# Decoder layer with attention, cross-attention and experts: two reorderings at the seams between its stages

## The chip, the core and the metric

The kernel runs on one core of one Trainium2 chip. The metric is the device time of one execution in microseconds (us). Its engines are named as the profile names them: PE (matrix multiplication; PEld is its weight load), DVE (vector), ACT (activation), POOL (GpSimd), and SP, which only issues DMAs. Matrices pass through PE as 32-bit floats, so each product of the program is two passes in the profile's counts (a transpose is one).

## What is computed

`x` is a batch of 8 sequences of 512 positions and 256 features. Three blocks follow each other, each adding its output to `x`:

```
x = x + attn(layernorm(x))                 # 16 heads, causal window of 128, 16 global positions
x = x + xattn(layernorm(x), ctx)           # 16 heads, 64 context positions, mask
x = x + ffn(layernorm(x))

def ffn(x):                                # S = 8, B = 512: attention over the 8 sequences
    y = layer_norm(x + mha(x), g1, be1)    # 4 heads
    idx = argmax(y @ Wg.T)                 # one of 8 experts for each of 4096 rows
    out = for each row: relu(y @ W1[idx] + b1[idx]) @ W2[idx] + b2[idx]
    return layer_norm(y + out, g2, be2)
```

The attention of the third block runs across the 8 sequences at one position, so it works on groups of 16 positions (8 x 16 = 128 rows).

## The kernel before

**Stages.** The first stage goes through the 8 sequences: self-attention and, one sequence behind, cross-attention. Each finished sequence is written to a DRAM tensor `x2d`; the last one in two halves (`HALVES`). The second stage, the blocks, takes 64 positions of all sequences at a time (`NBLK` = 8 blocks of `NG` = 4 groups): `block_start` loads nothing itself but normalises the rows and makes q, k and v, `group` is the attention of one group, `block_end` does the layer norm, the choice of the expert, and the scatter of each row to its expert's place in the DRAM tensor `rows_d`. The third stage, the expert tiles, takes 128 rows of one expert at a time: `expert_tile(i)` gathers them, loads W1, transposes, multiplies by W1 (L1281), takes the relu on ACT and DVE (L1286, L1288), multiplies by W2 (L1296), normalises and scatters to the output. It begins once the first four blocks are scattered and runs between the later groups.

**What sets the order.** Every piece of work is a Python generator that is started at a step number (`works`) and goes on to its next `yield` once a step (`in_steps`). What it yields is its rank in the next step: `PREFIX` 0, `TURN` 1, `VALUES` 2, `SMALL` 3, `SCORES` 4, `OTHER` 5, `EXPS` 6, `LOADS` 7; lower ranks come first, and among equals the piece begun last. The order so made is the order of each engine's queue: `in_order` adds a dependency from each instruction of PE, DVE, ACT and POOL to the one before it on its engine. SP's DMAs keep the program's order as well.

**The first seam.** The last half of the last sequence ends at steps `F0 + 1` to `F0 + 3` in `context_end`: the sums `den` (L723) on PE, three filler matmuls (`keep_busy(3)`, L286), the reciprocal `rd` on DVE (L732), a product that makes two columns of it, `rz`, on POOL (L735), its spreading over the partitions `ri` on PE (L750), the product `xoT` on DVE (L760), the output projection on PE (L198) and its sum on DVE (L446). Between these stands `block_start(0)`: it begins at step `F0`, does nothing in it, and in step `F0 + 1`, at rank `LOADS`, makes the statistics (`statistics`: L157, L159, L160 on DVE, the power on POOL at L161) and the normalised rows `fxn` (L168 on DVE), and issues the loads of block 2. In step `F0 + 2` come four filler matmuls (`keep_busy(4)`) and the transposes of `fxn` (L186), which ACT copies out (L188). Block 0's rows come by four loads of 112 rows each (L847) and one load of the last sequence's 16 rows for all groups (L852), which waits for the first half's write to `x2d`.

**The second seam.** Tile 0 begins at step `F0 + 35`. Its transposes (L1270) are in step `F0 + 37` and its first products (L1281) in step `F0 + 38`, at rank `EXPS`, so behind that step's group work on PE: the transposes of one group's probabilities (L983, which wait for POOL's product L978), another's values (L989), the experts' logits of block 5 (L1019) and the output projection of a third (L198). In the same step, at rank `TURN`, are tile 1's transposes. Ahead of the first products stands the read of the expert's number into a register of PE (L1274).

Of the kernel before, what the change touches and what calls it, by code (L numbers as in the profile page):

```python
# [41 lines left out]
PREFIX, TURN, VALUES, SMALL, SCORES, OTHER, EXPS, LOADS = range(8)  # L42
# [58 lines left out]
def decoder_kernel(ctx: ExitStack, tc: tile.TileContext, a: dict, out: bass.AP):  # L101
# [48 lines left out]
    def statistics(src):  # L150

        n = src.shape[1]
        st = small.tile([P, NG, 6], F32, tag="st")
        mv = small.tile([P, NG, 2], F32, tag="mv")
        rs = small.tile([P, NG], F32, tag="rs")
        for i in range(n):
            nc.vector.bn_stats(st[:, i, :], src[:, i, :])  # L157
        for i in range(n):
            nc.vector.bn_aggr(mv[:, i, :], st[:, i, :])  # L159
        nc.vector.tensor_scalar(rs[:, :n], mv[:, :n, 1], EPS, None, ALU.add)  # L160
        nc.gpsimd.tensor_tensor(rs[:, :n], rs[:, :n], nhalf[:, :n], ALU.pow)  # L161
        return mv, rs

    def normalised(dst, src, mv, rs, g=None, be=None):
        for i in range(src.shape[1]):
            m, r = mv[:, i, 0:1], rs[:, i : i + 1]
            if g is None:
                nc.vector.tensor_scalar(dst[:, i, :], src[:, i, :], m, r, ALU.subtract, ALU.mult)  # L168
            else:
                nc.vector.scalar_tensor_tensor(  # L170
                    dst[:, i, :], src[:, i, :], m, g, ALU.subtract, ALU.mult
                )
                nc.vector.scalar_tensor_tensor(
                    dst[:, i, :], dst[:, i, :], r, be, ALU.mult, ALU.add
                )
# [45 lines left out]
    if True:  # L221
# [60 lines left out]
        def keep_busy(n):  # L282

            ps = ps_m.tile([P, 512], F32, tag="m", name="busy_ps")
            for i in range(n):
                nc.tensor.matmul(  # L286
                    ps[:, : 2 * P], ident, cst[:, C_ID : C_ID + 2 * P], start=True, stop=True
                )

        def prepared():  # L290

            for t in (vc.rearrange("p b j d -> p (b j d)"), *vzs):
                nc.vector.memset(t, 0.0)
            nc.vector.tensor_copy(upto_q, cst[:, C_TRI : C_TRI + P])
            nc.vector.tensor_scalar(xbq4, xbq, 0.25, None, ALU.mult)

            nc.vector.tensor_copy(ident_b, ident)
            nc.vector.tensor_copy(
                pre_b, cst[:PRE, C_CUR : C_CUR + PRE].unsqueeze(1).to_broadcast([PRE, 8, PRE])
            )  # L300
            for r in range(2):
                half = slice(64 * r, 64 * r + 64)
                nc.vector.tensor_copy(
                    twice_b[half], cst[half, C_ID + 64 * r :][:, :NKC].unsqueeze(1).to_broadcast([NKC, 2, NKC])
                )
            nc.vector.tensor_copy(
                selx_b, cst[:, C_SELX : C_SELX + 2 * P].rearrange("p (f k) -> p f k", f=2)
            )
            for i in range(2):
                nc.gpsimd.memset(nxs[i], 0.0)  # L310

            keep_clock(1)
            yield

        def context_keys():
            for hf in range(2):
                ps = ps_m.tile([P, 512], F32, tag="m")
                project(ps, xwk, hf * P, ctxT)
                for r, mask in enumerate((mask_e, mask_o)):
                    nc.vector.tensor_scalar(  # L320
                        kc[:, hf, :, r, :],
                        ps.rearrange("p (b k) -> p b k", k=NKC),
                        xbk[:, hf : hf + 1],
                        mask,
                        ALU.add,
                        ALU.mult,
                    )
                yield

        def context_values(bs):  # L330
            for b in bs:
                ps = ps_m.tile([P, 512], F32, tag="m")
                for r in range(2):
                    heads = slice(r * HD, (r + 1) * HD)
                    for k in range(2):
                        nc.tensor.matmul(
                            ps[r * 64 : (r + 1) * 64, :P],
                            ctxT[:, k, b * NKC : (b + 1) * NKC],
                            xwv[:, k, :].rearrange("p (j d) -> p j d", d=2 * HD)[:, :, heads],
                            start=k == 0,  # L340
                            stop=k == 1,
                        )
                for r in range(2):
                    rows = slice(r * 64, (r + 1) * 64)
                    heads = slice(r * HD, (r + 1) * HD)
                    nc.vector.tensor_tensor(
                        vc[rows, b, :, heads],
                        ps[rows, :P].rearrange("p (j d) -> p j d", d=HD),
                        xbv[rows].rearrange("p (j d) -> p j d", d=2 * HD)[:, :, heads],
                        ALU.add,  # L350
                    )
                if b % 2:
                    yield
# [423 lines left out]
        F0 = START[B] + 9  # L777
# [3 lines left out]
        works = [(3, prepared(), LOADS), (5, context_keys()), (7, context_values(range(B)))]  # L781
# [17 lines left out]
    if True:  # L799
# [75 lines left out]
        def block_start(n):  # L875

            t = blocks[n]
            yr = t["yr"]
            x2 = yr[:, :, D : 2 * D]
            xn = one.tile([P, NG, D], F32, tag="xn", name=f"fxn_{n}")  # L880
            if n == 0:

                yield LOADS
            stats = statistics(x2)
            if n:
                yield
            normalised(xn, x2, *stats)
            if n + 2 < NBLK:
                block_load(n + 2)
            yield  # L890
            xT = one.tile([P, 2, 512], F32, tag="xT", name=f"fxT_{n}")
            if n == 0:
                keep_busy(4)
            transposed(xT, xn, ps_m)

            def add_bias(g):
                nc.gpsimd.tensor_tensor(yr[:, g, :D], xn[:, g], f["bo"], ALU.add)

            add_bias(0)
            add_bias(1)  # L900
            yield
            t["q"] = qT = qsh.tile([P, 2, 512], F32, tag="qT", name=f"fq_{n}")
            kT = qsh.tile([P, 2 * ROW], F32, tag="pT", name=f"fk_{n}")[:, : 2 * 512]
            t["k"] = kT = kT.rearrange("p (f q) -> p f q", f=2)
            for hf in range(2):
                ps = ps_m.tile([P, 512], F32, tag="m")
                project(ps, f["wqkv"], hf * P, xT)
                nc.scalar.activation(
                    qT[:, hf], ps, AF.Identity, bias=f["bq"][:, hf : hf + 1], scale=0.125
                )  # L910
                ps = ps_m.tile([P, 512], F32, tag="m")
                project(ps, f["wqkv"], D + hf * P, xT)
                nc.scalar.activation(
                    kT[:, hf], ps, AF.Identity, bias=f["bqkv"][:, 2 + hf : 3 + hf]
                )
                add_bias(2 + hf)
                yield
            t["v"] = v = qsh.tile([P, NG, D], F32, tag="pc", name=f"fv_{n}")
            for gg in range(NG // 2):
                ps = ps_m.tile([P, 2, D], F32, tag="m")  # L920
                for i in range(2):
                    project_rows(ps[:, i, :], f["wqkv"], 2 * D, xT, (2 * gg + i) * P)
                nc.vector.tensor_tensor(
                    v[:, 2 * gg : 2 * gg + 2],
                    ps,
                    f["bv"].unsqueeze(1).to_broadcast([P, 2, D]),
                    ALU.add,
                )
            nc.gpsimd.tensor_copy(
                yr[:, :, 2 * D], cst[:, C_TOK + n * NG : C_TOK + (n + 1) * NG]  # L930
            )
# [281 lines left out]
        def expert_tile(i):  # L1213
# [56 lines left out]
                nc.tensor.transpose(pt[:, k, :], t[:, k * P : (k + 1) * P], ident)  # L1270
            tT = tsh.tile([P, 2, P], F32, tag="rT", name="tT")
            nc.vector.tensor_copy(tT, pt)
            yield EXPS
            e_pe = nc.tensor.value_load(eidx[0:1, j : j + 1], min_val=0, max_val=E - 1)  # L1274
            h = one.tile([P, NG, D], F32, tag=("xn", "xT")[i % 2], name=f"h_{i}")
            h = h.rearrange("p g d -> p (g d)").rearrange("p (f t) -> p f t", t=P)
# [46 lines left out]
        works += [(F0 - 18, block_weights()), (F0 - 6, norm_weights()), *((F0 - 5, block_loads(n)) for n in range(2))]  # L1323
        works += [(F0 + 5, made_room(), LOADS), (F0 + 9, expert_weights())]
        for n in range(NBLK):
            works.append((F0 + 4 * n, block_start(n)))
            for g in range(NG):
                works.append((F0 + 4 * n + 6 + g, group(n, g)))
            works.append((F0 + 4 * n + 15, block_end(n, 0, NG)))
        for k, (nb, n) in enumerate(((NB1, NT1), (NB2, NT2 - NT1), (NBLK, NT - NT2))):  # L1330
            works.append((F0 + 4 * nb + 16, make_table(f"t{k}", n, nb < NBLK)))
        for i in range(NTC):
            works.append((F0 + 4 * NB1 + 19 + i, expert_tile(i), VALUES))
# [109 lines left out]
```

## Time and profile before

| | |
|---|---|
| median of 3 runs | 1115.96 us (1115.93 to 1119.26) |
| the profiled execution's own time | 1115.88 us |
| its span, first to last instruction | 1114.1 us |
| busy: PE, DVE, ACT, POOL | 1047.9, 712.5, 580.3, 474.0 us |
| share of PE in the chain that ended last | 54% |
| the first seam, 603.0 to 617.8 us | PE busy 13.1 of 14.8 us |
| the second seam, 806.0 to 819.6 us | PE busy 11.0 of 13.6 us |

A line of a timeline gives the start in us from the span's start, the us to the end of the last of its instructions, the engine, the line of the kernel, the operation, the tile written and those read, the shapes, the count, and in brackets how long the engine was idle before it and what ended that. Ends of matmuls are modelled and overlap the next start, so the time between two starts tells more than a length. A view by stretches gives for each stretch its length, each engine's busy us with the number of its instructions, the clock granted to PE as a share of full speed, the busy share of the DMA engines and the GB/s. A releaser is inferred from semaphores. Lines are those of the kernel before; in the changed kernel they are one less from L888 on.

### The profile page before, as it was taken

How to read it: one execution, taken by the hardware profiler on the slowest of the kernel's cores; microseconds unless marked ns; L12 is line 12 of the kernel's file. 1: busy time of each engine (PE TensorE's matmuls, PEld its weight loads, DVE VectorE, ACT ScalarE, POOL GpSimd, SP SyncE). 2: the span in 40 equal slices, each digit the busy share in tenths (PEclk: the TensorE clock that was granted, in tenths of full speed). 3: DMA queues.
4: the chain of work that ended last, by engine and by line, in shares of the span. 5: the costliest groups of instructions: out<-in, count | busy, mean ns of one | idle time of the engine just before them, and what ended most of it. 6: DMA issues, size and time to landing. Idle time of an engine off the chain costs nothing.

```text
span 1114.1 us, 24420 instructions
## 1 busy us (share of the span) xinstructions
PE 1047.9 (94%) x8940; PEld 764.8 (69%) x8940; DVE 712.5 (64%) x1809; ACT 580.3 (52%) x2039; POOL 474.0 (43%) x553
## 2 busy tenths in 40 slices
PE   9798998999989999899999999999899999999994
PEld 5465665566655666666656577666678999999993
DVE  6958668497584874857853445667756675544542
ACT  2878678677686677766842456555431211111110
POOL 2152424235243262333421333455465766555552
PEclk9999999999999999999999999999999999999997
DMA  6000001010010010100003660121466877666630
GB/s 219 11 1 11 2 1 49 1 48 2 1 49 2 21 30 1 48 11 21 30 10 100 192 174 2 39 76 39 143 201 201 260 231 251 213 202 210 197 112 10
DMA packets 55824, 95.31 MB, mean 86 GB/s; under 512 B 11282, under 2 KB 39189, under 8 KB 55704
## 3 DMA queue, kind: packets, MB, share of 16 engines
q1 hardware_dynamic: 48408, 72.71, 21.1%
q0 software_dynamic: 7296, 21.02, 5.7%
q8 instruction: 73, 1.20, 0.4%
q14 instruction: 47, 0.39, 0.1%
HBM read 78.22 MB, written 17.45 MB: 86 GB/s over the span
## 4 chain that ended last, share of the span: by engine, by line
PE 54%; DVE 20%; ACT 8%; issue 4%; DMA 4%; POOL 2%; POOLq 0%; DVEq 0%; SPq 0%
PE ps L193 11%; PE hps L1281 9%; PE ps L1296 8%; PE ps L198 8%; ACT s L515 5%; DMA tb<-rows_d,t2srci 4%; DVE s L503 3%; DVE nm L511 2%; PE av L574 2%; DVE rx L530 2%; DVE nm L647 2%; PE ps L952 2%; PE xav L711 2%; PE sc L467 1%; DVE xb L446 1%
## 5 line engine op out<-in xcount | busy, mean ns | idle before, releaser
L515 ACT ACTIVATE s<-s,nm 128x144 f32<-128x144 f32 (+1 forms) x512 | 203.4, 408 | 9.2 <-DVE nm L511 9.2
L1286 ACT ACTIVATE h<-hps,b 128x128 f32<-128x128 f32 x148 | 42.3, 368 | 212.8 <-issue 184.2
L1281 PE MATMUL hps<-tT,w 128*128 128x128 f32 x1184 | 138.6, 275 | 0.1
L1281 PEld LDWEIGHTS hps<-tT,w 128*128 128x128 f32 x1184 | 135.5, 192 | 0.6 <-DMA r<-in_b 0.3
L551 POOL TENSOR_TENSOR pc<-pT,cst 128x512 f32<-128x512 f32 x96 | 123.0, 1302 | 30.4 <-DVE pT L547 29.8
L1296 PE MATMUL ps<-w,h 128*128 x592 | 133.7, 379 | 0.0
L1296 PEld LDWEIGHTS ps<-w,h 128*128 128x128 f32 x592 | 109.7, 190 | 13.4
L515 ACT ACTIVATION_READ_ACCUMULATOR s<-s,nm 128x1 f32 x512 | 101.0, 197 | 0.0
L526 POOL COPY rx<-s 128x128 f32<-128x128 f32 x48 | 14.6, 305 | 198.9 <-ACT s L515 198.9
L161 POOL TENSOR_TENSOR rs<-rs,nhalf 128x4 f32<-128x4 f32 (+1 forms) x34 | 33.5, 985 | 132.2 <-DVE rs L160 131.5
L511 DVE TENSOR_REDUCE nm<-s 128x8 f32<-128x1152 f32 (+1 forms) x64 | 84.5, 1320 | 5.5
L1288 DVE TENSOR_SCALAR h<-hps,b 128x128 f32<-128x128 f32 x148 | 41.7, 345 | 66.1 <-ACT h L1286 66.1
L467 PE MATMUL sc<-kz,qT 32*128 32x512 f32 (+1 forms) x512 | 76.0, 593 | 3.0 <-DVE s L495 2.3
L503 DVE COPY_PREDICATED s<-upto_q,sc 128x512 f32<-128x512 int32 x96 | 65.0, 731 | 19.5 <-ACT s L502 19.5
L545 PE MATMUL pt<-cst,s 128*128 128x128 f32 x512 | 72.0, 277 | 2.4 <-ACT pT L549 1.7
L502 ACT COPY s<-sc 128x512 f32<-128x512 f32 x96 | 51.7, 592 | 39.2 <-PE sc L467 39.2
L545 PEld LDWEIGHTS pt<-cst,s 128*128 128x128 f32 x512 | 59.0, 142 | 17.8 <-issue 6.9
L193 PE MATMUL ps<-fxT,w_fwqkv 128*128 128x512 f32 x128 | 58.8, 604 | 0.0
L193 PE MATMUL ps<-xT,w_wqkv 128*128 128x512 f32 x128 | 58.2, 597 | 0.0
L978 POOL TENSOR_TENSOR fs<-fs,sm 128x512 f32<-128x512 f32 x32 | 33.3, 1041 | 57.7 <-DVE sm L977 53.6
L529 DVE RECIPROCAL rc<-sm 128x8 f32<-128x8 f32 x64 | 12.6, 197 | 69.4 <-ACT s L515 69.2
L1310 POOL TENSOR_TENSOR rs<-rs,nhalf 128x1 f32<-128x1 f32 x37 | 21.5, 580 | 75.4 <-DVE rs L1309 59.6
(249 smaller groups left out, 2241.4 us busy)
## 6 DMA issues: line engine op xcount, KB each, us to landing
w<-in_W SPq DMA_DIRECT2D x45, 1024.0 KB
r<-in_b SPq DMA_DIRECT2D x37, 128.0 KB
xb<-in_x SPq DMA_DIRECT2D x7, 512.0 KB
x2d<-xb SPq DMA_DIRECT2D x7, 512.0 KB
y<-x2d SPq DMA_DIRECT2D x24, 128.0 KB
mj<-in_maskT SPq DMA_DIRECT2D x16, 128.0 KB
cst<-in_consts SPq DMA_DIRECT2D x1, 1011.0 KB
y<-x2d SPq DMA_DIRECT2D x8, 112.0 KB
```

What stands on the lines that cost most here:

```text
L193: nc.tensor.matmul(ps, w[:, k, o0 : o0 + P], xT[:, k, :], start=k == 0, stop=k == 1)
L198: nc.tensor.matmul(ps, xT[:, k, t0 : t0 + P], w[:, k, o0 : o0 + D], start=k == 0, stop=k == 1)
L467: nc.tensor.matmul(ps[j // 2][:, j % 2].rearrange("p r w k -> p r (w k)"), qT[rows[j], hf, q0 : q0 + P], kz[rows[j], hf, :, q0 + P - nw * ...
L502: nc.scalar.copy(s4, ps[jj][:, :, :, 0, :])
L503: nc.vector.copy_predicated(s4, upto_q.unsqueeze(1).unsqueeze(1).to_broadcast([P, 2, 2, P]), ps[jj][:, :, :, 1, :],)
L511: nc.vector.tensor_reduce(nm, s[:, :, :nk], AX.X, ALU.max, negate=True)
L515: nc.scalar.activation(s[:, h, :nk], s[:, h, :nk], AF.Exp, bias=nm[:, h : h + 1], accum_out=sm[:, h : h + 1],)
L545: nc.tensor.transpose(pt[:, h, :], s[:, 4 * jj + h, :P], ident)
L551: nc.gpsimd.tensor_tensor(pc[:, hs, :], pT[:, hs, :], upto_k.unsqueeze(1).to_broadcast([P, 4, P]), ALU.mult,)
L1281: nc.tensor.matmul(ps[:, f, :], w1[:, k, f * P : (f + 1) * P], tT[:, k, :], start=k == 0, stop=k == 1)
L1286: nc.scalar.activation(h[:, f, :], ps[:, f, :], AF.Relu, bias=b1[:, f : f + 1])
L1296: nc.tensor.matmul(ps, h[:, f, :], new["w2"][:, bass.ds(e_pe, 1), f, :].rearrange("p o d -> p (o d)"), start=f == 0, stop=f == NFC - 1,)
```

## The change

The first block's generator starts one step earlier, makes its statistics in step `F0`, yields, and normalises one step later, so the statistics stand ahead of the reciprocal of the last sums in DVE's queue, and the power ahead of `rz` in POOL's. Two of the four filler matmuls ahead of its transposes go. The first expert tile's generator yields `TURN` in place of `EXPS` ahead of its first products, so these stand behind tile 1's transposes and ahead of the groups' work of that step; its relu parts on ACT and DVE and its two sums on POOL (L1291, L1292) move ahead in their queues with them. The other blocks and tiles keep their ranks.

```diff
@@ block_start
             stats = statistics(x2)
-            if n:
-                yield
+            yield OTHER if n else LOADS
             normalised(xn, x2, *stats)
             if n + 2 < NBLK:
                 block_load(n + 2)
             yield
             xT = one.tile([P, 2, 512], F32, tag="xT", name=f"fxT_{n}")
             if n == 0:
-                keep_busy(4)
+                keep_busy(2)
             transposed(xT, xn, ps_m)
@@ expert_tile
             nc.vector.tensor_copy(tT, pt)
-            yield EXPS
+            yield EXPS if i else TURN
             e_pe = nc.tensor.value_load(eidx[0:1, j : j + 1], min_val=0, max_val=E - 1)
@@ works
         for n in range(NBLK):
-            works.append((F0 + 4 * n, block_start(n)))
+            works.append((F0 + 4 * n - (n == 0), block_start(n)))
```

## Prediction

> **What bounds the kernel now.** I read the page first, then the timelines of PE, DVE and POOL around the two places that the diff touches, then the stretches with their granted clock, then the landings of DMAs.
>
> The page gives PE 94% of the span:
>
> ```profile
> span 1114.1 us, 24420 instructions
> ...
> PE 1047.9 (94%) x8940; PEld 764.8 (69%) x8940; DVE 712.5 (64%) x1809; ACT 580.3 (52%) x2039; POOL 474.0 (43%) x553
> ```
>
> From 608 us to 1098.6 us, PE's last matmul, PE stands still for few moments of over 0.06 us; two clusters of them lie at the edits. A microsecond saved there reaches the end only if nothing behind it is late instead. The profiled execution took 1115.88 us, 1.78 more than its span, and the median of the three runs is 1115.96; I sum against 1115.88 and add 0.08.
>
> The first place, PE and then DVE (start, us, engine, line, tile, shape, count, idle before and what ended it):
>
> ```profile
> 606.67 1.92 PE L723 MATMUL den<-xp,cst 128*32 128x128 f32 x32
> 608.52 1.56 PE L286 MATMUL busy_ps<-cst 128*128 128x256 f32 x6
> 610.47 1.13 PE L750 MATMUL ri<-rz,cst 64*128 64x256 f32 x4 [0.39 <-POOL rz L735]
> 611.53 1.99 PE L286 MATMUL busy_ps<-cst 128*128 128x256 f32 x8
> 613.36 0.54 PE L186 MATMUL xps<-cst,fxn 128*128 128x128 f32 x2
> 614.30 0.33 PE L186 MATMUL xps<-cst,fxn 128*128 128x128 f32 x1 [0.41 <-DVE fxn L168]
> 615.03 0.76 PE L186 MATMUL xps<-cst,fxn 128*128 128x128 f32 x5 [0.40 <-DVE fxn L168]
> 615.85 1.97 PE L198 MATMUL ps<-w_xwo,xoT 128*128 128x256 f32 x8
> ```
>
> ```profile
> 608.70 0.96 DVE L732 RECIPROCAL rd<-den 64x128 f32<-64x128 f32 x1 [6.59 <-PE den L723]
> 609.70 1.41 DVE L157 BATCH_NORM_STATS2 st<-y 128x6 f32<-128x256 f32 x4
> ...
> 611.41 0.17 DVE L160 TENSOR_SCALAR rs<-mv 128x4 f32<-128x4 f32 x1
> 612.78 2.20 DVE L168 TENSOR_SCALAR fxn<-y,mv,rs 128x256 f32<-128x256 f32 x4 [1.19 <-POOL rs L161]
> 615.01 0.69 DVE L760 TENSOR_TENSOR xoT<-ri,xoT 128x512 f32<-128x512 f32 x1
> ```
>
> DVE stood idle for 6.59 us before the reciprocal, and then had the reciprocal, the statistics and the normalisation to do one behind the other while PE spent 1.83 us on filler (L286) and still waited 0.81 us for the normalised rows.
>
> The second place, PE, and the stretches with the clock (stretch; length; busy us and counts of PE, PEld, DVE, ACT, POOL; granted clock; DMA):
>
> ```profile
> 809.69 0.38 PE L1270 MATMUL pt<-cst,tb 128*128 128x128 f32 x2
> 812.29 0.70 PE L983 MATMUL pt<-cst,fs 128*128 128x128 f32 x4 [2.22 <-POOL fs L978]
> ...
> 816.53 3.73 PE L1281 MATMUL hps<-tT,w 128*128 128x128 f32 x32
> 820.10 0.38 PE L1270 MATMUL pt<-cst,tb 128*128 128x128 f32 x2
> ```
>
> ```profile
> 809.40:812.80 3.40, 1.18 (x9) 0.75 (x7) 1.12 (x5) 0.26 (x1) 2.97 (x4) 1.00 0.41 157
> 812.80:816.20 3.40, 3.40 (x29) 2.35 (x28) 0.00 (x0) 2.62 (x11) 2.61 (x3) 0.50 0.33 64
> ```
>
> PE waits 2.22 us for POOL, whose queue is full of scatters, and in the next 3.4 us its clock is granted at half, so that the groups' matmuls (L983 to L198) take 4.24 us instead of 2.66 (0.53 + 0.59 + 0.57 + 0.97, the same lines at 767.68 to 770.34). Tile 0's products then stand behind all that.
>
> **Part 1: block 0's statistics ahead of the reciprocal.** In the changed program's order only DVE's block of statistics moves past L732, POOL's L161 past L735, and two of four filler matmuls go; SP's order is the same. block_load(2) and its four DMAs keep their place.
>
> The statistics may start when block 0's last load lands. SP issues it at 604.70 and the trace's last landing record of it is at 606.96. L157 to L160 took 609.70 to 611.58, 1.88 us, with 0.05 of overlap at the end, so now 606.98 to 608.86. The denominators (L723) end at 608.66, so the reciprocal is held for some 0.1 us: 608.81 to 609.77. POOL's L161 starts 0.15 us after L160 and takes 1.01: 609.01 to 610.02. The pair L735, which used to start at 609.81, now has L161 ahead of it and starts at 610.05, 0.24 later; so `ri` starts at 610.71 instead of 610.47 (PE's wait there grows from 0.39 to 0.63) and ends at 611.77. The two fillers left take half of 1.83, to 612.69. L168 starts when L161 is done, at 610.06 instead of 612.78, and with 2.20 us ends at 612.26: all four rows are there before the fillers end, so PE's waits of 0.41 and 0.40 go. Eight transposes at 1.02 (L186 x8 elsewhere) end at 613.71; L760 follows L168 on DVE, 612.26 to 612.95, ahead of that. L198 starts at 613.71 instead of 615.85: **2.14 us**. What is late next is PE itself. The removed fillers cost nothing: what they covered is gone. If the rows were late by x, PE would wait x less the 0.43 us between 612.26 and 612.69. Bounds of this part: 0 if the load lands 2.1 us later, and 2.4 if POOL's order cost nothing.
>
> From 617 to 804 us PE is idle only at 777 and at 785 to 788, both behind DVE work that itself follows PE, so the 2.14 us travel on.
>
> **Part 2: tile 0's products ahead of the groups.** On PE the 16 products (L1281, 32 passes, 3.57 us) move from behind L198 to right behind tile 1's transposes, ahead of L983, L989, L1019 and L198. ACT's L1286 moves ahead of L984, L997, the last group's exponentials (L969) and L1029; DVE's L1288 ahead of L1002; POOL's L1291 and L1292 (0.73 + 0.68 us) ahead of a memset and a gather. Times below are on the scale of the profile of before.
>
> What the products wait for is there: tT at 809.04, W1 (landed at 787.9), the PSUM pair (exponentials done at 808.59). New is that PE's first read of the expert's number, L1274, is no longer hidden behind matmuls: its sequencer work ran from 814.01 to 815.50, 1.49 us. Begun behind tile 1's transposes, at about 809.2, it lets the products start at about 810.8; PE idles 0.7 us instead of 2.22. For the cost of this uncovered read there are two ends, nothing and the whole 1.49 behind 810.07 (811.56); either is inside the slack found below.
>
> Products 810.8 to 814.4; the four groups' lines at full clock 2.66 us, to 817.0. Then tile 2's transposes need their gather, landed at 817.17 (0.13 us to PE as at tile 0): 817.30. Then L983 needs POOL's product L978, 816.67 to 817.72, which no part of the change moves, since POOL works from 808.87 on without a PE wait: L983 at 817.78 instead of 820.32. From there to the next products took 2.62 us with an ACT wait of 0.21, of which I keep 0.1, since ACT no longer has L1286 in front: 817.78 + 2.27 is 820.05 for PE's tile 1 products, instead of 822.94: **2.89 us**. PE has 0.5 to 0.8 us in hand before POOL's 817.72, so neither the register read nor the half clock of a passing wait is needed for this number.
>
> Who is behind the new waits: ACT holds L984 to L1029 for L1286 (814.4 to 815.5), so the last exponentials end at 817.8 instead of 816.0; their reciprocal and POOL's L978 come at 821 to 822, before 822.86 to 823.9 of now. DVE's L1288 waits for ACT to 815.5 with L1002 behind it, whose matmul only ends at 817.0. The gather behind L1291 and L1292 lands at about 823.5 instead of 821.94, and is used at 827 (829.97 less 2.9). W1 of tile 2 lands at 825.9, used at 830.
>
> A rule to weigh against this: the Trainium skill, "TensorE: Matmul & The Clock Gate", Part 1, has PE fall to half clock after an idle window of about 3.4 us, and advises only against gaps longer than about 3 us. By that rule a wait of 2.22 us would not have cost the clock; the row shows that it did (busy 1.18 of 3.40, then 0.50). What follows if the half clock has another cause is a rival below.
>
> **Sum.** 1115.88 - 2.14 - 2.89 + 0.08 = 1110.9.
>
> **Rivals.**
> - *The half clock stays*, because it comes from where PE's evaluation falls and not from this wait (for it: at 505.6 the clock also is 0.50 behind a stretch in which PE was busy 2.85 of 3.40). Then 14 of the 32 passes and part of the groups' lines behind 812.8 take twice their time, about 1.7 us, less the 0.5 of slack: part 2 gives 1.7, and the time is 1112.1.
> - *A later transfer takes it back.* PE is nearly gapless behind 843 us, but tile 11's gather lands at 898.23 and is used at 898.88. If gathers there go by DMA traffic and not by PE, up to 5.0 - 0.65 = 4.4 us would return: 1111 to 1115.3, middle 1113. Against it: gathers wait for buffers that PE and DVE free, so they move too.
> - *The load is late* (the slower side). DVE takes its instructions in order: all of part 1 hangs on the load being down before the denominators. L198 starts 6.73 us after the statistics. At a landing of 609.1 part 1 is worth nothing (1113.0), at 612.0 it has eaten part 2, and behind that the kernel is slower: it would need 7.3 us from issue instead of the 2.26 traced. W1 loads in a full queue take up to 9.7 us (822.66 to 832.38), but here the queue ahead is empty.
> - *The change does not move what it says*: the program's order shows that it does, so only noise would be left, 1115.9.
>
> **How the numbers follow.** Forecast 70%, half clock 10%, transfer 9%, load late 8% (half of it still faster, a third slower), no effect 3%. Three runs spread by 3.3 us once, so I take 0.3% (3.3 us) as what can be told from no change: faster means below 1112.6. The forecast and most of the half-clock case lie there, 0.78; slower 0.03; the rest 0.19. Range: below, POOL not binding in part 2 (0.7 more) and 0.2 in part 1 give 1110.0; above, the half clock and the middle of the transfer case give 1113.5.
>
> **What would show it.** In the profile of the changed kernel: DVE's L157 about 0 to 0.2 us behind the landing and L732 behind it, `ri` 0.2 later, no wait at the first block's transposes, L198 2.1 us earlier; at the second place PE's largest wait under 1 us, granted clock 1.00 all through, L983 of tile 2's stage released by POOL, products of tile 1 5.0 us earlier than now; and the same 5 us at PE's last matmul. It is wrong if L732 starts over 0.5 us after the denominators, if the clock shows 0.50 there, or if a gap behind 843 us has grown.

## The result, and the profile after

The changed kernel took 1112.76 us in the median of ten runs (1108.94 to 1115.53), the kernel before 1115.95 us in the median of ten beside it (1112.96 to 1119.26). The ratio is 0.9966, with a 95% interval of 0.9954 to 0.9979. The means lie 3.3 ± 0.9 us apart. The profiled execution of the changed kernel took 1111.08 us, the third shortest of its ten, and 4.80 less than the profiled one of before (1115.88).

The page of the changed kernel:

```profile
span 1109.2 us, 24414 instructions
...
PE 1045.7 (94%) x8936; PEld 764.3 (69%) x8936; DVE 712.9 (64%) x1809; ACT 579.7 (52%) x2039; POOL 474.1 (43%) x553
```

PE has the same share of a span that is 4.9 us shorter; its work has hardly changed (four passes of filler less), so what went was waiting and slow clock.

The first seam of the changed kernel, PE and then DVE (columns as in the prediction):

```profile
606.31 1.92 PE L723 MATMUL den<-xp,cst 128*32 128x128 f32 x32
608.15 1.56 PE L286 MATMUL busy_ps<-cst 128*128 128x256 f32 x6
610.48 1.13 PE L750 MATMUL ri<-rz,cst 64*128 64x256 f32 x4 [0.77 <-POOL rz L735]
611.54 1.13 PE L286 MATMUL busy_ps<-cst 128*128 128x256 f32 x4
612.51 1.04 PE L186 MATMUL xps<-cst,fxn 128*128 128x128 f32 x8
613.38 1.89 PE L198 MATMUL ps<-w_xwo,xoT 128*128 128x256 f32 x8
```

```profile
606.75 1.41 DVE L157 BATCH_NORM_STATS2 st<-y 128x6 f32<-128x256 f32 x4 [5.01 <-DMA y<-x2d]
...
608.67 0.96 DVE L732 RECIPROCAL rd<-den 64x128 f32<-64x128 f32 x1
609.77 2.59 DVE L168 TENSOR_SCALAR fxn<-y,mv,rs 128x256 f32<-128x256 f32 x4
```

The statistics now fill part of what was a wait of 6.59 us on DVE, the eight transposes follow each other without a wait, and L198 starts 5.16 us behind the denominators' end (608.22) instead of 7.26. The wait ahead of `ri` has grown from 0.39 to 0.77.

The second seam, PE, then POOL's product that the last L982 waits for, and two stretches around tile 0's products (columns as in the prediction):

```profile
807.14 0.38 PE L1269 MATMUL pt<-cst,tb 128*128 128x128 f32 x2
808.20 3.81 PE L1280 MATMUL hps<-tT,w 128*128 128x128 f32 x32 [0.67 <-issue]
...
815.22 0.66 PE L982 MATMUL pt<-cst,fs 128*128 128x128 f32 x4
...
817.52 3.73 PE L1280 MATMUL hps<-tT,w 128*128 128x128 f32 x32
```

```profile
814.12 1.05 POOL L977 TENSOR_TENSOR fs<-fs,sm 128x512 f32<-128x512 f32 x1
```

```profile
806.90:810.30 3.40, 2.73 (x23) 2.42 (x23) 1.07 (x5) 0.21 (x1) 2.93 (x4) 1.00 0.42 159
810.30:813.70 3.40, 3.40 (x45) 2.86 (x44) 0.49 (x2) 1.66 (x6) 2.66 (x3) 1.00 0.41 66
```

The wait of 2.22 us is gone, 0.67 us in front of the products has come, and the clock is 1.00 throughout. L982 of tile 2's stage starts 0.05 us behind the end of POOL's product (815.17): in this execution POOL is now what PE follows.

Where the time went, between PE's starts of the instructions named (us):

| piece | before | after |
|---|---|---|
| PE's first matmul to the denominators (L723) | 605.22 | 604.86 |
| first seam: L723 to block 0's first L193 | 10.98 | 8.80 |
| to tile 1's transposes | 192.04 | 192.03 |
| second seam: tile 1's transposes to its products | 13.25 | 10.38 |
| to the end of PE's last matmul | 275.69 | 276.22 |

The two seams give 5.05 us. 0.53 is lost again behind them, 0.37 of it at 835.85, where the wait of L988 for DVE's L1001 grew from 0.44 to 0.81. The 0.36 gained ahead of the first seam lies where the change does nothing.

### The profile page after: what moved, and what is told of

Its sections match the earlier page's. It is cut to its first block, busy times and chain, and to the rows that moved or that the text cites. A ratio compares the mean times of both kernels' runs of the same rounds, so it can differ in the third digit from the quotient of the medians.

```text
span 1109.2 us, 24414 instructions
## 1 busy us (share of the span) xinstructions
PE 1045.7 (94%) x8936; PEld 764.3 (69%) x8936; DVE 712.9 (64%) x1809; ACT 579.7 (52%) x2039; POOL 474.1 (43%) x553
## 4 chain that ended last, share of the span: by engine, by line
PE 55%; DVE 20%; ACT 7%; DMA 5%; issue 4%; POOL 1%; POOLq 0%; DVEq 0%; SPq 0%
PE ps L193 11%; PE hps L1280 9%; PE ps L1295 9%; PE ps L198 7%; ACT s L515 5%; DMA tb<-rows_d,t2srci 4%; DVE s L503 3%; DVE nm L511 2%; PE av L574 2%; DVE rx L530 2%; DVE nm L647 2%; PE ps L951 2%; PE sc L467 2%; DVE xb L446 2%; DVE pT L547 1%
## 5 line engine op out<-in xcount | busy, mean ns | idle before, releaser
L1295 PEld LDWEIGHTS ps<-w,h 128*128 128x128 f32 x592 | 109.8, 190 | 13.3
L161 POOL TENSOR_TENSOR rs<-rs,nhalf 128x4 f32<-128x4 f32 (+1 forms) x34 | 33.5, 985 | 144.3 <-DVE rs L160 143.3
L193 PE MATMUL ps<-fxT,w_fwqkv 128*128 128x512 f32 x128 | 58.8, 604 | 0.0
L193 PE MATMUL ps<-xT,w_wqkv 128*128 128x512 f32 x128 | 58.2, 598 | 0.0
L977 POOL TENSOR_TENSOR fs<-fs,sm 128x512 f32<-128x512 f32 x32 | 33.4, 1042 | 55.8 <-DVE sm L976 53.6
```

Source lines behind the costliest of these rows:

```text
L193: nc.tensor.matmul(ps, w[:, k, o0 : o0 + P], xT[:, k, :], start=k == 0, stop=k == 1)
L1295: nc.tensor.matmul(ps, h[:, f, :], new["w2"][:, bass.ds(e_pe, 1), f, :].rearrange("p o d -> p (o d)"), start=f == 0, stop=f == NFC - 1,)
```

## Experiments

Runs of one comparison ran on one chip, with the kernel before among them. The spread of single times is wide (2 us standard deviation), and it goes with the execution's mean granted clock. So beside the mean difference the tables give that at equal clock: one straight line of time against clock for all kernels of a comparison (0.72 and 0.69 us per 0.001), and the distance between kernels along it. Errors there are standard errors. What a change saves by way of the clock itself is left out of the value at equal clock and is in the plain mean.

**1. Each part alone.** `e0_both` is the changed kernel. `e1_part1` has the first seam's change with the old second one, `e2_part2` the reverse:

```diff
 e1_part1, against the changed kernel
-            yield EXPS if i else TURN
+            yield EXPS
 e2_part2, against the kernel before
-            yield EXPS
+            yield EXPS if i else TURN
```

> The changed kernel again, on the chip and beside the runs of before that the three parts share. Two stretches are read from each trace: seam 1 from the start of the sums (L723, the last 32 passes of it) to the first projection of block 0 (L193), 10.98 us in the kernel before (606.67 to 617.65); seam 2 from tile 1's transposes to tile 1's products, 13.25 us (809.69 to 822.94). My theory: 8.8 and 10.4 in every execution, no half clock in seam 2, and a mean time 3.5 to 5 us under that of before. Rival (the gain is taken back behind 843 us): the two stretches shorter by 5 us and the last PE instruction earlier by under 3.

> Only block 0's statistics are moved (and two fillers gone); tile 0's products stay behind the groups. My theory: seam 1 is 8.8 us, seam 2 has its wait of 2.2 us for POOL and is 11.7 us when the clock stays full and 13.3 when a stretch of 3.4 us falls on the wait and the clock is halved after it; mean time 2.1 us under before, so a ratio of 0.998. Rival (the parts do not add up, because one buys what the other would): more than 3 or less than 1 us.

> Only tile 0's products are moved; block 0 starts as before with its four fillers. My theory: seam 1 stays at 11.0, seam 2 is 10.4 us with the clock at 1.00, its end set by POOL's product L978; mean time 1.3 us under before where before's clock stays full in seam 2 and 2.9 where it is halved, so a ratio of 0.9975 to 0.999. Rival (a uncovered register read and ACT's relu ahead of the last exponentials cost what the wait gave): seam 2 at 12 to 13.

Repeated on another chip:

> The changed kernel once more, on whatever chip, beside part 2 alone. Theory A (part 2 is worth the whole 2.89 us only in executions in which tile 0's gather comes early and PE then waits 2.22 us for POOL; where the gather is late that wait is short and part 2 is worth next to nothing): 2.5 to 3.8 us under the kernel before in the mean over many executions, 3 to 3.8 at equal granted clock. Theory B (both terms in every execution): 5.0 under it. First seam 8.8, tile 0's transposes to tile 1's products 14.8 to 15.7.

> Only tile 0's products moved, again. Theory A: 0.5 to 1.8 us under the kernel before in the mean, about 1.3 at equal granted clock. Theory B: 2.9 under it. First seam 11.0, tile 0's transposes to tile 1's products 14.8 to 15.7.

| run (12 executions each) | median us | ratio to before, 95% | mean difference | at equal clock | first seam | second seam |
|---|---|---|---|---|---|---|
| e0_both | 1114.88 | 0.9981 [0.9965, 0.9997] | -2.8 ± 0.8 | -3.4 ± 0.4 | 8.84 | 10.09 |
| e1_part1 | 1115.32 | 0.9991 [0.9971, 1.001] | -1.3 ± 0.9 | -2.4 ± 0.4 | 8.82 | 10.00 |
| e2_part2 | 1116.75 | 1.0005 [0.9991, 1.0018] | -0.6 ± 0.6 | -1.3 ± 0.4 | 10.99 | 10.27 |
| e0b_both | 1114.72 | 0.9961 [0.9946, 0.9976] | -3.8 ± 0.6 | -4.5 ± 0.3 | 9.67 | 9.37 |
| e2b_part2 | 1116.84 | 0.9995 [0.998, 1.0011] | -1.0 ± 0.5 | -1.6 ± 0.3 | 10.98 | 10.68 |

(Before: 1117.08 in the first comparison, 1117.95 in the second.) The first seam is as expected in four of the five traces; in e0b_both a halved clock stretch falls on the denominators, which take 2.99 us instead of 1.92, and 0.2 of that comes back as in e5_four below. The means of e0_both and e1_part1 are below what was expected of them (2.8 against 3.5 to 5, and 1.3 ± 0.9 against 2.1). At equal clock the parts add up: 2.4 and 1.3 against 3.4, and the second chip leaves 3.0 for part 1 and 1.6 for part 2. So part 1 is worth its 2.1 us or somewhat more, and part 2 about half of the 2.87 that one trace showed. The plain means, which count the clock, put part 2 no higher (0.6 and 1.0, each ± 0.6). The second seam in e1_part1 was expected at 11.7 or 13.3 and took 10.00, with part 2 absent: there PE came to tile 1's transposes late, through a halved stretch just ahead (808.1 to 811.5), and the wait for POOL was 0.39 us.

**2. The first seam: what carries it.** `e3_fillers` is the kernel before with `keep_busy(2)` for `keep_busy(4)`, `e5_four` the changed kernel with `keep_busy(4)`, `e6_none` the changed kernel without that filler:

```diff
 e3_fillers, against the kernel before
-                keep_busy(4)
+                keep_busy(2)
 e5_four, against the changed kernel
-                keep_busy(2)
+                keep_busy(4)
 e6_none, against the changed kernel
-            if n == 0:
-                keep_busy(2)
```

> The kernel before with two of the four filler matmuls (L286) gone and the order as it was. Theory: the fillers only cover the wait for the normalised rows, so PE waits 0.92 us more there, 1.7 in all instead of 0.81, and the first seam stays at 10.98. Rival (the gain at the first seam comes from the fillers that went): 10.07, and L198 starts 6.35 us behind the denominators' end instead of 7.26.

> The changed kernel with four fillers as before. Theory: with the statistics early PE itself is what is late, so the two more fillers cost what they take, 0.92 us: L198 starts 6.08 us behind the denominators' end (5.17 in the changed kernel, 7.26 before), the first seam is 9.72. Rival (normalised rows or L760 still bound): 8.8.

> The changed kernel with no filler matmul at the first seam. Theory: two normalised rows are there when PE has finished the reciprocals' product (ri), the others come every 0.65 us, and then L198 waits for L760, which ends 0.7 us behind the last row: L198 starts about 4.9 us behind the denominators' end instead of 5.17, the first seam is 8.5, and the time cannot be told from that of the changed kernel (0.3 us). Rival (PE's longer idle there halves its clock): first seam 9.5 to 10.5, and about 1 us over the changed kernel in executions whose clock stretch falls so.

PE of e3_fillers:

```profile
611.50 0.56 PE L186 MATMUL xps<-cst,fxn 128*128 128x128 f32 x2 [0.68 <-DVE fxn L168]
612.46 0.33 PE L186 MATMUL xps<-cst,fxn 128*128 128x128 f32 x1 [0.40 <-DVE fxn L168]
613.20 0.77 PE L186 MATMUL xps<-cst,fxn 128*128 128x128 f32 x5 [0.41 <-DVE fxn L168]
```

The fillers that went became 0.68 us more of wait, and L198 starts 7.26 us behind the denominators' end, to the hundredth as before: fewer fillers alone give nothing. (Its first seam is 12.40, since a halved stretch begins at 614.4; one trace cannot tell whether the longer wait ahead of it brought that about.) In e5_four L198 starts 5.81 us behind that end where 6.08 was expected, and its first seam is 10.51. The denominators themselves ran at half clock there and ended 1.05 us later, so that POOL's L161 was done before the reciprocal and `ri` came 2.05 us behind them instead of 2.26. That 0.2 fits the price of L161 ahead of L735, which shows only when the denominators are on time; with it the two fillers cost what they take. e6_none: 4.95 us, first seam 8.70, no halved stretch there; 1114.57 us, ratio to before 0.9964 [0.9948, 0.998], which can't be told from e0b_both.

`e7_late_load` is the changed kernel in which SP issues block 2's four loads ahead of block 0's last one:

```diff
             for _ in range(4):
                 yield
+            if n == 0:
+                block_load(2)
             nc.sync.dma_start(
...
-            if n + 2 < NBLK:
+            if 0 < n < NBLK - 2:
                 block_load(n + 2)
```

> The changed kernel with the four loads of block 2 issued ahead of block 0's last load, each 0.6 to 0.75 us on SP's queue, so that this load lands some 2.6 to 3 us later. Theory (DVE takes its instructions in order, the statistics hold the reciprocal): L157 starts 0.0 to 0.2 us behind the landing, L732 only behind L160, and L198 some 6.7 us behind L157's start; with the landing 0.8 to 1.4 us behind the denominators' end, L198 starts 7.5 to 8.1 us behind that end: part 1 is lost and up to 0.8 us more. Rival (the load is not what the statistics wait for, or the reciprocal goes ahead): 5.2 as in the changed kernel.

DVE, PE, and the granted clock in three stretches of it:

```profile
614.79 1.41 DVE L157 BATCH_NORM_STATS2 st<-y 128x6 f32<-128x256 f32 x4 [9.80 <-DMA y<-x2d]
...
616.71 0.96 DVE L732 RECIPROCAL rd<-den 64x128 f32<-64x128 f32 x1
```

```profile
618.52 2.07 PE L750 MATMUL ri<-rz,cst 64*128 64x256 f32 x4 [5.56 <-POOL rz L735]
```

```profile
611.80:615.20 3.40, 1.16 (x6) 0.68 (x4) 0.41 (x2) 0.00 (x0) 0.00 (x0) 1.00 0.49 156
615.20:618.60 3.40, 0.08 (x1) 0.08 (x1) 3.20 (x12) 0.00 (x0) 1.63 (x2) 0.50 0.17 55
618.60:622.00 3.40, 3.40 (x8) 2.29 (x9) 2.49 (x5) 0.00 (x0) 2.22 (x3) 0.50 0.00 0
```

The load landed 4.5 us behind its issue (610.19 to 614.70; 2.26 in the prediction), because four loads stood ahead of it, and so it was later than expected: 3.2 us behind the denominators' end (611.46). The statistics start with the landing, the reciprocal stands behind them, and L198 starts 9.30 us behind L157 instead of 6.63, since PE idled for 5.56 us and its clock is halved from 615.2 to 625.4. The first seam takes 16.93 us: 8.1 over the changed kernel, 4.8 of it by the later statistics, 2.7 up to L198 and 0.7 behind it. One execution took 1123.39 us; as two of the kernel before on that chip took 1123.04 and 1118.73, single times decide nothing here (e3_fillers 1118.82, e5_four 1115.79).

**3. The second seam: the wait and the clock.** `e4_gap_filled` is the kernel before with five filler matmuls behind tile 1's transposes; `b_again` the kernel before unchanged; `e9_late_gather` the kernel before with four more memsets on POOL ahead of tile 0's gather:

```diff
 e4_gap_filled
+            if i == 1:
+                keep_busy(5)
 e9_late_gather
-                nc.gpsimd.memset(t, 0.0)
+                for _ in range(5 if i == 0 else 1):
+                    nc.gpsimd.memset(t, 0.0)
```

> The kernel before, with five filler matmuls (10 passes of 0.23 us) behind tile 1's transposes, where PE waited 2.22 us for POOL; nothing is moved. It tells the wait from the half clock behind it. My theory: the half clock came from the wait, so the clock is 1.00 in seam 2, the groups' lines take 2.7 us and not 4.2, and seam 2 is 11.7 us instead of 13.25, though the wait is only filled and not used. Rival (the half clock falls where it will): 13.25 with a stretch at 0.50, or 11.7 only by luck, as in a kernel whose wait is left open.

> The kernel before, unchanged, in another execution. Theory A (how long PE waits for POOL at the second seam hangs on how late tile 0's gather is): PE's wait at tile 0's transposes and its wait ahead of L983 behind tile 1's transposes trade against each other, since POOL's row of scatters runs by its own time; where the first is over 1.4 us (0.75 in the first profile), the second is under 1.2 us (2.22 there), the halved stretch falls elsewhere or not at all, and tile 0's transposes to tile 1's products take 15 to 16.5 us instead of 18.4. Theory B (the 2.22 us and the half clock are in every execution): 18.4 again, with 0.50 in the stretch behind the wait. The first seam is 10.98 by both (12.0 if a halved stretch falls into it).

> The kernel before with four more memsets of tile 0's rows (0.53 us each) on POOL ahead of its gather, so that the gather is issued up to 1.5 us later, less where it waits for the scatters anyway. Theory A (POOL's own row of work, from its L978 behind tile 0's second gather on, sets when tile 2's groups can start; PE's waits only trade places): PE waits about 2 us at tile 0's transposes, the wait ahead of L983 behind tile 1's transposes shrinks from 2.22 to about 0.7 or less, tile 0's transposes to tile 1's products take 15 to 16.9 us instead of 18.4, and from block 0's first L193 to tile 1's products it is 205.3 or less. Rival (each wait adds to the other): the wait of 2.22 stays, 18.4, and 206.8.

| old order | PE's wait at L983 | clock in the seam | second seam |
|---|---|---|---|
| before; b_again; e3_fillers | 2.22 each | 0.50 behind the wait | 13.25; 13.27; 13.29 |
| e9_late_gather | 2.22 | 1.00 | 11.86 |
| e4_gap_filled | 0 (0.30 ahead of 2.43 of filler) | 1.00 | 12.18 |
| e1_part1 | 0.39 | 1.00 (0.50 just ahead) | 10.00 |

The six traces with tile 0's products first and no halved stretch at or just ahead of the seam took 10.09 to 11.09, 10.52 in the mean. The stretch that holds the wait and the one behind it, in b_again (L983 starts at 814.97) and then in e9_late_gather (818.65):

```profile
812.15:815.55 3.40, 1.18 (x8) 0.70 (x7) 1.04 (x5) 0.19 (x1) 2.90 (x4) 1.00 0.41 157
815.55:818.95 3.40, 3.40 (x28) 2.48 (x28) 0.00 (x0) 2.62 (x11) 2.69 (x3) 0.50 0.40 49
```

```profile
814.95:818.36 3.41, 1.48 (x10) 1.09 (x8) 1.92 (x8) 1.21 (x4) 2.81 (x3) 1.00 0.29 111
818.36:821.77 3.41, 3.12 (x35) 2.26 (x36) 0.00 (x0) 2.36 (x10) 2.78 (x4) 1.00 0.39 64
```

The same wait was followed by a halved clock in one trace and not in the other. Halved stretches come in pieces of 3.41 us, and where they begin differs from execution to execution (812.8, 815.6, 815.7 for this one). In the three traces in which the whole wait fell into one such piece (busy 1.18), the next was halved; in e9_late_gather, by the pieces counted on from its halved one at 606.7, 1.93 us of it did (busy 1.48), and the clock stayed. Busy time alone does not decide it, though. In e0b_both a piece with 1.65 us busy (805.02 to 808.43) was followed by a halved one. Pieces with 2.24 us busy near 785 us, cut at other instructions from trace to trace, were followed by one in e2b_part2, e4_gap_filled and e6_none, and not in the profiles of before and after, in e0_both and in e2_part2. So the rule behind the halving is not shown. By these traces the old order costs 11.86 - 10.52 = 1.3 us by the wait (one trace against six), and 1.4 more in executions that get the halved stretch. e4_gap_filled has no halved stretch in the seam either, and took 12.18 where 11.7 was expected, because the five fillers take 2.43 us, two passes each, and hold L983 0.40 us past POOL's product. It gains 1.1 us in the seam against b_again and yet is slower over many executions, 1.0017 [1.0002, 1.0033], 1.7 ± 0.6 us in the mean and 0.9 ± 0.4 at equal clock. What costs it that is open, so its times do not confirm the price of the halved clock.

Theory A of b_again and e9_late_gather fell: the wait does not trade against that for tile 0's gather. PE waited 0.75 us for that gather in before, nothing in b_again and e3_fillers, and 1.23 in e9_late_gather, and the 2.22 stayed; in e9_late_gather the memsets also made POOL's own row late. (From tile 0's transposes to tile 1's products it took 19.3 us in b_again, more than the 18.4 of Theory B, and 16.8 in e9_late_gather, which lies in Theory A's range, but by the full clock.) POOL's L978 (L977 in e1_part1) ahead of tile 1's gather and the PE rows behind it, in before and then in e1_part1:

```profile
802.84 1.04 POOL L978 TENSOR_TENSOR fs<-fs,sm 128x512 f32<-128x512 f32 x1 [1.43 <-DVE sm L977]
807.89 1.09 PE L186 MATMUL xps<-cst,y 128*128 128x128 f32 x8 [0.32 <-DVE y L1002]
```

```profile
803.61 1.04 POOL L977 TENSOR_TENSOR fs<-fs,sm 128x512 f32<-128x512 f32 x1 [0.79 <-DVE sm L976]
810.45 1.57 PE L186 MATMUL xps<-cst,y 128*128 128x128 f32 x8
813.50 0.63 PE L982 MATMUL pt<-cst,fs 128*128 128x128 f32 x4 [0.39 <-POOL tb L1226]
```

In before, b_again, e3_fillers and e9_late_gather, L983 (at 812.29 in before) starts 9.45 us behind the start of that L978, and PE's transposes L186 5.05 us behind it: the 2.22 is a fixed distance between POOL's row and the row that PE follows. It shrank only where PE was late by itself, in e1_part1 (L186 at 6.84). Theory A of e0b_both and e2b_part2 rests on the same trade. The means of both and the 1.6 of part 2 agree with its numbers; the 4.5 of e0b_both at equal clock lies between its 3.8 and Theory B's 5.0. From tile 0's transposes to tile 1's products e0b_both took 15.6 us as expected, and e2b_part2 16.5 where at most 15.7 was.

## Why the prediction was right, point by point

- **Part 1, 2.14 us: right.** The trace gives 2.10 at L198 and 2.18 over the seam, and e3_fillers, e5_four and e7_late_load show that the order carries it. The wait for `ri` grew a little more than predicted (0.77 against 0.63), since the statistics began 1.47 us ahead of the denominators' end and not 1.68, and held the reciprocal to 0.45 us behind that end, just inside the 0.5 that I named.
- **Part 2, 2.89 us: right for the profiled execution, too large for most.** Its intermediate times held: products 1.06 us behind tile 1's transposes (1.1), L982 of tile 2 at 8.08 (8.09), tile 1's products at 10.38 (10.36), L982 released by POOL. The term that was mis-sized is the clock's: I put "in the next 3.4 us its clock is granted at half" into the price of the wait for every execution, though it held in three traces with the wait of 2.22 us and not in the fourth. Over many executions part 2 is worth 1.3 to 1.6 us at equal clock, and 0.6 to 1.0 (± 0.6) in the plain mean. One step was close: I gave the gather behind L1291 and L1292 3.5 us in hand (823.5, "used at 827"). In the trace it landed 7.2 us behind its issue (817.27 to 824.50) and was used at 824.64, so 0.14 us were left.
- **The register read.** "Nothing and the whole 1.49" were its ends, and both came: products started without a wait in e0b_both and e5_four (PE at half clock just ahead), after 0.35 to 0.72 us in five traces, and after 1.49 in e2b_part2. It cost little, as predicted, because of what PE meets at tile 2. In the changed kernel's first profile and in e0_both that is POOL's product (L982 0.05 us behind its end). In e0b_both, e2_part2, e6_none and e7_late_load it is tile 2's gather, for which PE waits 0.26 to 1.08 us, so that L982 starts 0.35 to 0.82 us behind the product; in the prediction the gather landed 0.55 us ahead of the product's end. In e2b_part2 PE itself comes 0.34 us behind the product, and in e5_four, whose clock is halved to 814.1, PE is 2.21 us behind the product.
- **The sum.** 1110.9 against 1111.08 for the profiled execution and 1112.76 for the median: a gain of 5.03 us predicted, 4.80 traced, 2.8 to 3.8 in the means. That the traced one comes so near is in part luck: the profile of before had the halved stretch behind its wait, and 0.36 gained ahead of the seams and 0.53 lost behind them nearly cancel.
- **The rivals.** *Half clock stays*: not in this trace, but its price for part 2 (1.7) is close to what many executions give, for another reason than the one named. *A later transfer takes it back*: no; tile 11's gather cost nothing, and of the 0.53 lost behind the seam all but 0.05 lies ahead of 839 us. *The load is late*: it did not happen, and e7_late_load shows the mechanism with the price short by 2.7 us, since I left out the halved clock, which there followed PE's wait of 5.56 us. *The change does not move what it says*: no.

Open: why part 2 shows less in the plain mean than at equal clock. If it spared a halved stretch in some executions, the mean clock would rise; it is 0.9885 and 0.9887 against 0.9895 and 0.9894 (each ± 0.0006). Whether halved stretches come elsewhere instead, the traces are too few to say.

## What to carry to other kernels

When an in-order engine sits idle ahead of one late instruction, look for work queued behind it whose inputs have landed, and price that work's own input being late: here the move gave 2.1 us, and a load 3.2 us late cost 8.1. Price a wait and the halved clock behind it apart: here the wait was 2.22 us in four of the five traces that left it open, and a halved stretch followed it in three of these four. And where one execution's trace shows a slow stretch, look for it in a second before it goes into a sum.

## What the runs showed of the hardware

- **The clock's pieces.** All halved stretches ahead of PE's last matmul are one to three times 3.41 us long, and the same code was hit in one execution and spared in the next: with one kernel, 431.05 to 437.88 in the profiled execution and nothing between 36 and 1097 us in e0_both. The Trainium skill, "TensorE: Matmul & The Clock Gate", Part 1, has a free-running window of 3413 ns that does not begin anew with the kernel: the traces agree. The same part of the Trainium skill has the clock fall after an idle window of about 3.4 us. The traces differ: the clock was halved behind pieces with 1.18 us of 3.40 busy, and at times behind pieces with more.
- **From profile to profile.** From the issue of the last scatter ahead of the reload of a row buffer (L1079) to that reload's issue, which waits for it, it took 7.2 and 7.1 us in the first two profiles and 7.8 to 8.9 in the later ones, which ran on three chips; on which the first two ran is not on record. There DVE waits up to 1.62 us for a block's rows in its statistics (e0_both, 752.06), and block 0's L193 to tile 0's transposes took 188.3 to 191.1 us instead of 186.9 and 186.8, with either order. That is 4.3 us more in e0_both, whose profiled execution is no faster than the one in the result although it has 6.8 us less of halved clock. That the chip makes the difference, and that the late loads bring about the whole of it, is not shown.
